# A four-layer transformer kernel: transposes a step behind their normalisation, the residual later, and the gated FFN's statistics and pieces placed elsewhere

## The chip, the cores and the metric

The kernel runs on one core of a Trainium2 chip. The metric is the device time of one execution in microseconds (us). The core has five engines that matter here: TensorE (PE, with its weight loads PEld), VectorE (DVE), ScalarE (ACT), GpSimd (POOL), and SyncE (SP), whose queue issues the DMA transfers. Each engine runs its own instructions in its program's order and waits on semaphores for the others.

## The reference

The input x has 2 sequences of 2048 rows of 256 floats (4096 rows). Four residual layers follow each other, each on a layer norm of the rows:

```python
x = x + A(layernorm(x))   # pre-norm attention, 16 heads of 16 over 4 key heads, causal window 64, rope; then FFN 256-1024-256 with gelu
x = x + B(layernorm(x))   # two layers of local attention and gated FFN
x = x + C(layernorm(x))   # gated attention unit: silu(uv), relu(q k + bias)**2, linear
x = x + D(layernorm(x))   # linear with a weight quantised to -1, 0, 1

# A(x): h = ln(x) * g1 + b1; x = x + attention(h) @ Wo + bo
#       x = x + gelu((ln(x) * g2 + b2) @ Wf1 + bf1) @ Wf2 + bf2
# a layer of B, twice:
h = shift_token(x)                   # second half of the columns from the row before
q, k, v = split(h @ wqkv, 3)         # 8 heads of 64
q, k = rotary_xpos(l2norm(q) * qs, l2norm(k) * ks)
x = x + local_attention(q, k, v) @ wo            # window 128, looks one window back
h = layernorm(shift_token(x)) * lg + lb
a, g = split(h @ w1 + b1, 2)         # 682 each
x = x + (a * gelu(g)) @ w2 + b2
```

All of it is in 32-bit floats.

## The kernel before, in words

**Tiling.** The rows are 32 tiles of 128 (NT). Four tiles make a group (GT = 4, NG = 8); a whole group is loaded, normalised and put through an FFN together. The rows stay on the chip in R through stage B; weights are loaded stage by stage.

**Steps.** Stages A and B are each a software pipeline in steps, one tile a step. A table says what each step holds: at(step, what, ...) appends an entry, and step_a and step_b write out the instructions of one step from its entries. For tile t, the projection to q, k, v stands in step t, scores in t+1, softmax weights (A: attend) in t+2, output (B: values and output) in t+3. In A, group g is loaded in step 4g-5, its statistics (means_of, L145 and L146) stand in 4g-3, and its normalisation in 4g-2. A's first layer norm is taken twice, the outer of the residual layer and the inner of the attention block: statistics_twice computes both scales in one POOL power (L161); normalised_twice makes h on DVE (L170); normalised_once makes y, the outer norm, which is the row sum that attention and FFN are added to, on DVE (L179) and ACT (L184); add_rows adds the bias bo to y on POOL (L207). to_features transposes h on PE (L215) and evicts it on ACT with gain and shift (L220); the projection (L380) reads that.

**FFN pieces.** When a group's attention is done, its FFN is prepared in step s = 4(g+1)+3: statistics, normalisation (A: L198), transposes. The products follow as pieces in later steps: in A eight hidden ones (L552) and four outputs (L563), in B six hidden (L1147, with the gate L1162 and L1163 on ACT and DVE) and four outputs (L1170, added by L1177). fill0, fill1 and fill2 are the places in a step where pieces stand. In A, finish closes a group five steps after s (the statistics and normalisation for B).

**Order.** The loop runs inside manual_schedule for PE, ACT, DVE and POOL: these four execute in the order in which step_a and step_b write their instructions. Only SP's queue, which carries the loads, is ordered by the framework's planner; in the trace SP issues transfers out of the program's order. The loop step is s; B's step is s - JOINT with JOINT = 35, so that A's tail (the last group's FFN) runs beside B's first steps. That is the joint A to B. Layer 1 of B starts GAP steps after layer 0's last tile: the joint of the layers.

**A step of B,** in the order of the program: values and their eviction (L1046, L1058 on PE; L1068 ACT, L1069 DVE); scores (L968), maxima (L980, L987 on DVE); exponentials (L999, ACT); projection (L893, PE), its evictions (L905, L907, ACT); turn, the rotated halves' products (L914 and L917, POOL); rotate_mul (L937, DVE); norm: sum of squares (L929, DVE), maximum and power (L930 and L932, POOL); rotate_add (L940, DVE); fill0; scale_keys (L944, DVE); softmax division (L1007, L1010, DVE); output (L1075) and its add (L1080); transposes of the softmax weights (L1018, L1023) with their evictions (L1030, L1032); to_features of q and k (L949, PE), the second half of which reads what L944 wrote; fill1 and fill2. In a prepare step the Ffn's parts are added: shifted (four DMA transfers of the rows' second halves, one row on, and in layer 1 a load xr of the residual), statistics (L1113 to L1115 on DVE, then rstd_of: L135 and L137 on POOL), normalise (eight of L1123 on DVE), residual (L1131 on POOL, four adds, eight in layer 1) and to_features (L215).

The lines around which the prepare step turns:

```python
if "prepare" in todo:
    l, g = todo["prepare"][0]
    f = ffns[l, g] = Ffn(l, g, wts[l])
    sh = f.shifted(sh)
    f.statistics()
...
if f:
    f.normalise()
if p:
    p.rotate_mul(0)
```

Scratch memory is divided into regions by address (W_B, LOW, HIGH, W_A); tags that are given to the region low share it between stages.

Of the kernel before, what the change touches and what calls it, by code (L numbers as in the profile page):

```python
# [12 lines left out]
ALU = mybir.AluOpType  # L13
# [4 lines left out]
P = 128  # L18
# [3 lines left out]
GT = 4  # L22
# [23 lines left out]
def kernel(ctx: ExitStack, tc: tile.TileContext, I: dict, out: bass.AP):  # L46
# [102 lines left out]
    def statistics_twice(src):  # L149

        mv = means_of(src)
        ve = T(small, [P, 2, GT], "ve2")
        nc.vector.tensor_scalar_add(ve[:, 0, :], mv[:, :, 1], EPS)
        nc.vector.tensor_scalar(ve[:, 1, :], mv[:, :, 1], 1.0 + EPS, EPS * EPS, ALU.mult, ALU.add)
        rs = T(small, [P, 2, GT], "rs2")  # L160
        nc.gpsimd.tensor_tensor(  # L161
            rs, ve, mhalf[:, 0 : 2 * GT].rearrange("p (a b) -> p a b", a=2), ALU.pow
        )
        return mv, rs

    def normalised_twice(src, stats, dst):
# [38 lines left out]
    def add_rows(dst, rows):  # L205
        for t in range(GT):
            nc.gpsimd.tensor_add(dst[:, t, :], dst[:, t, :], rows(t))  # L207
# [61 lines left out]


    low = Region(LOW, HIGH)
    low_tags = {tag: low for tag in ("y1", "xr1", "h", "hT2", "G")}
    wa = Region(HIGH + 5184, W_A, 2, low_tags)
    ca = wa
# [4 lines left out]
    class GroupA:  # L279
# [10 lines left out]
        def normalise(self):  # L290
            self.h = T(wa, [P, GT, D], "h", 1)
            normalised_twice(self.xg, self.stats, self.h)
            self.y = T(wa, [P, GT, D], f"y{self.g % 3}", 1)
            normalised_once(self.xg, self.stats, self.y, residual=False)
            add_rows(self.y, lambda t: boA)

        def to_features(self):
# [293 lines left out]
        at(t + 2, "attend", t)  # L591
        at(t + 3, "output", t)
    for g in range(NG):
        at(GT * g - 5, "load", g)
        at(GT * g - 3, "statistics", g)
        at(GT * g - 2, "normalise", g)
        s = GT * (g + 1) + 3
        at(s - 1, "residual", g)
        at(s, "prepare", g)

        if g < NG - 1:
            for c in range(ADFF // P):
                at(s + 1 + c // 4, f"fill{c // 2 % 2}", g, "hidden", c)
            for tt in range(GT):
                at(s + 3 + tt // 2, f"fill{tt % 2}", g, "output", tt)
        at(s + 5, "finish", g)

    groups_a, tiles_a, ffns_a = {0: first_group}, {}, {}
    steps_a = steps
# [1 line left out]
    def step_a(todo):  # L611
# [37 lines left out]
        if q:  # L649
            q.scores()  # L650
            q.mask(0)
            q.mask(1)
        if p:
            p.project()
            p.take()
# [39 lines left out]
            o.add_output()  # L695
        if q:
            q.exponents()
        if m:
            m.to_features()
        if f:  # L700
            f.to_features()


    wC = Region(W_A, END)
# [78 lines left out]


    low = Region(LOW, HIGH)
    wb = Region(HIGH + 5120, W_A, 2, {tag: low for tag in ("sh", "xr", "h", "hT", "gl", "hh")})
    cb = kept
    wb.reserve("tab", [P, 4, GT, BHD])
# [391 lines left out]

    GAP = 2
    steps = {}

    def at(step, what, *args):
# [6 lines left out]
    for l in range(BL):  # L1193
        s0 = l * (NT + GAP)
        for t in range(NT):
            at(s0 + t, "project", l, t)
            at(s0 + t + 1, "scores", l, t)
            at(s0 + t + 2, "weights", l, t)
            at(s0 + t + 3, "values", l, t)
            if t % GT == 0:  # L1200
                at(s0 + t - 4, "tables", l, t // GT)
                at(s0 + t - 3, "begin", l, t // GT)
        for g in range(NG):
            s = s0 + GT * (g + 1) + 3
            at(s, "prepare", l, g)

            for step, place, what, i in (
                (1, 0, "hidden", 0), (1, 1, "hidden", 1), (2, 0, "hidden", 2), (2, 1, "hidden", 3),
                (3, 0, "hidden", 4), (3, 0, "hidden", 5), (3, 1, "output", 0),
                (4, 0, "output", 1), (4, 1, "output", 2), (4, 2, "output", 3),  # L1210
            ):
                at(s + step, f"fill{place}", l, g, what, i)
        at(s0 + NT - 1, "free_qkv", l)
        at(s0 + NT + 2, "free_wo", l)
        at(s0 + NT + 7, "free_ffn", l)
# [1 line left out]
        at((BL - 1) * (NT + GAP) + NT + 3 + i, "next_stage")  # L1217


    for c in range(ADFF // P):  # L1220
        at(s_a + 1 + c // 4, f"fill{c // 2 % 2}", None, NG - 1, "hidden", c)
    for tt in range(GT):
        at(s_a + 3 + tt // 2, f"fill{tt % 2}", None, NG - 1, "output", tt)

    weights = {}
    wts = {0: weights}
# [5 lines left out]
    def step_b(todo):  # L1232
# [16 lines left out]
            tabs[l, g] = load_tab(g, scales[l])  # L1249
        if "prepare" in todo:  # L1250
            l, g = todo["prepare"][0]
            f = ffns[l, g] = Ffn(l, g, wts[l])
            sh = f.shifted(sh)
            f.statistics()

        def fill(place):

# [22 lines left out]
        if q:  # L1280
            q.scores(0)
            q.scores(1)
            q.maxima(0)
            q.maxima(1)
            q.exponents(0, (0,))
        if p:
            p.project(0)
# [2 lines left out]
            p.turn(0)  # L1290
        if q:
            q.exponents(0, (1,))
        if f:
            f.normalise()
        if p:
            p.rotate_mul(0)
            p.take(1)
# [14 lines left out]
        if p:  # L1312
            p.scale_keys()
        if f:
            f.residual()
        for l, g in todo.get("tables", ()):
            scale_tab(tabs[l, g], scales[l])
# [28 lines left out]
            groups[l, g] = begin_b(g, groups[l, g - 1][1] if g else None)  # L1346
        for r in rest:
            r()
        for (l,) in todo.get("free_qkv", ()):
            if l + 1 < BL:  # L1350
                wts[l + 1] = load_qkv(l + 1)
# [12 lines left out]
    with tc.manual_schedule(engines=ENGINES):  # L1364
        for s in range(min(steps_a), JOINT + max(steps) + 1):
            if s in steps_a:
                step_a(steps_a[s])
            if GT < s < JOINT - 4:
                next(masks, None)
            if s == JOINT + s_a + 6:  # L1370
                nc.gpsimd.memset(hh[:, 5, :], 0.0)
            step_b(steps.get(s - JOINT, {}))

# [340 lines left out]
```

## Time and profile before

| | us |
|---|---|
| median of 3 runs (lowest, highest) | 2650.28 (2650.09, 2653.59) |
| the profiled execution | 2653.07 |
| its span | 2651.3 |
| busy in the span: PE | 2578.8 |
| DVE | 1617.3 |
| ACT | 1197.5 |
| POOL | 985.8 |

The mean granted TensorE clock is 0.99. Stage A fills the first 510 us, B's projection starts at 513.28, B's last add (L1177) is at 1865.7, and C with D follow to the end. In the profile's rows a line number is that of the kernel before; "out<-in" are the program's names; a bracket holds the idle time of the engine just ahead of the instruction and what ended it. A line of the waits names the engine, the waiting instruction's output and line, what it waited for, and then the total in us, the number of times and the longest. A window's row has its bounds, its length, the busy time of PE, PEld, DVE, ACT and POOL with instruction counts, the granted clock, the DMA engines' busy share and GB/s. A helper's line (L135, L145, L215, L220) can serve several callers.

### The profile page before, as it was taken

The page shows a single profiled execution, that of the slowest core. Times are in us where ns is not written, and L with a number is a line of the kernel's source. Part 1 is how long each engine was busy: PE and PEld are TensorE (multiplying, and loading weights), DVE is VectorE, ACT ScalarE, POOL GpSimd, SP SyncE. Part 2 cuts the span into 40 slices and gives each one's busy share as a digit, 9 for nine tenths or more (in the row PEclk, how much of TensorE's full clock was granted, in tenths as well). Part 3 has the DMA queues.
Part 4 walks back from the last instruction along what each step waited for, and adds up shares of the span by engine and source line. Part 5 has one row for each costly group of instructions (what it writes and reads, how often), then busy time and mean ns, then how long its engine had stood idle before and what let it go on. Part 6 is the DMA issues. An engine that isn't in the chain of part 4 may idle for free.

```text
span 2651.3 us, 51289 instructions
## 1 busy us (share of the span) xinstructions
PE 2578.8 (97%) x20130; PEld 1647.1 (62%) x20130; DVE 1617.3 (61%) x4357; ACT 1197.5 (45%) x2505; POOL 985.8 (37%) x1221
## 2 busy tenths in 40 slices
PE   6899999998999999999999999999999999999998
PEld 4577777666666666666666676666545445445567
DVE  6778777567766767756766677774433435434344
ACT  3555555375666666646666666663510001500000
POOL 5555555544434444434544545542200002300011
PEclk9999999998999999999999999999999999999999
DMA  5001111111000001111210111001100000100000
GB/s 170 17 31 32 32 39 32 47 33 51 25 19 23 25 25 29 41 35 41 77 32 23 29 33 37 25 17 58 40 8 4 6 7 12 44 0 6 5 10 13
DMA packets 73168, 82.02 MB, mean 31 GB/s; under 512 B 18829, under 2 KB 57056, under 8 KB 72672
## 3 DMA queue, kind: packets, MB, share of 16 engines
q1 hardware_dynamic: 72928, 78.75, 10.4%
q8 instruction: 160, 2.62, 0.4%
q14 instruction: 80, 0.66, 0.1%
HBM read 44.20 MB, written 10.50 MB: 21 GB/s over the span
## 4 chain that ended last, share of the span: by engine, by line
PE 87%; DVE 5%; POOL 4%; issue 3%; DMA 1%; ACT 0%; SPq 0%; POOLq 0%; DVEq 0%; ACTq 0%
PE ps L1567 16%; PE ps L893 10%; PE ps L1147 10%; PE ps L1170 5%; PE ps L1491 4%; PE ps L563 4%; PE ps L552 4%; PE ps L1075 4%; PE ps L968 3%; PE ps L1046 2%; PE ps L1510 2%; PE ps L1479 2%; PE ps L1469 2%; PE ps L949 2%; PE ps L476 2%
## 5 line engine op out<-in xcount | busy, mean ns | idle before, releaser
L1567 PE MATMUL ps<-room 128*128 128x512 f32 (+1 forms) x1152 | 463.2, 544 | 0.0
L1567 PEld LDWEIGHTS ps<-room 128*128 128x128 f32 x1152 | 217.8, 189 | 221.9 <-issue 214.7
L893 PE MATMUL ps<-room 128*128 128x512 f32 x768 | 346.8, 601 | 0.0
L999 ACT ACTIVATE room<-room,shift,rn 128x192 f32<-128x192 f32 x512 | 276.4, 548 | 78.8 <-DVE shift L987 78.8
L914 POOL TENSOR_TENSOR room<-room 128x256 f32<-128x256 f32 x128 | 107.8, 842 | 493.1 <-ACT room L905 493.1
L1147 PE MATMUL ps<-room 128*128 128x512 f32 x640 | 287.7, 593 | 0.4 <-ACT room L220 0.4
L1535 ACT COPY room<-ps 128x256 f32<-128x256 f32 x32 | 11.9, 370 | 587.9 <-PE ps L1533 587.9
L932 POOL TENSOR_TENSOR rn<-ss,mhalf 128x8 f32<-128x8 f32 x128 | 243.0, 1898 | 10.7
L893 PEld LDWEIGHTS ps<-room 128*128 128x128 f32 x768 | 140.8, 190 | 157.4 <-issue 149.2
L1497 DVE SCALAR_TENSOR_TENSOR room<-ps,room 128x512 f32<-128x512 f32 (+1 forms) x144 | 90.2, 627 | 206.4 <-PE ps L1491 206.4
L1147 PEld LDWEIGHTS ps<-room 128*128 128x128 f32 x640 | 118.8, 190 | 136.8 <-issue 132.0
L1520 POOL TENSOR_SCALAR veC<-mvC 128x1 f32<-128x1 f32 x32 | 7.2, 226 | 453.5 <-DVE mvC L1518 453.5
L1170 PE MATMUL ps<-room 128*128 128x256 f32 x768 | 173.6, 380 | 0.0
L980 DVE CUSTOM_DVE_ANT_0 room<-ps,room 128x192 f32<-128x192 f32 x512 | 152.2, 354 | 15.7 <-PE ps L968 15.4
L1170 PEld LDWEIGHTS ps<-room 128*128 128x128 f32 x768 | 144.3, 191 | 24.9 <-issue 6.9
L1010 DVE TENSOR_SCALAR room<-room,rdB 128x192 f32<-128x192 f32 x512 | 156.1, 369 | 4.5
L1163 DVE SCALAR_TENSOR_TENSOR room<-ps,room 128x512 f32<-128x512 f32 x96 | 72.1, 751 | 127.1 <-PE ps L1147 88.7
L466 POOL TENSOR_TENSOR room<-room,mxA 128x1024 f32<-128x1024 f32 x64 | 120.2, 1900 | 58.4 <-PE ps L428 45.4
L1491 PE MATMUL ps<-room 128*128 128x512 f32 (+1 forms) x288 | 133.4, 545 | 0.0
L929 DVE TENSOR_REDUCE ss<-room 128x8 f32<-128x512 f32 x128 | 81.7, 680 | 73.9 <-ACT room L907 73.9
L1075 PE MATMUL ps<-room 128*128 128x256 f32 x512 | 121.0, 379 | 0.0
L1075 PEld LDWEIGHTS ps<-room 128*128 128x128 f32 x512 | 97.3, 190 | 34.1 <-issue 22.7
(182 smaller groups left out, 5019.9 us busy)
## 6 DMA issues: line engine op xcount, KB each, us to landing
room<-room SPq DMA_DIRECT2D x144, 128.0 KB
room<-in_L_attn_x_dram SPq DMA_DIRECT2D x16, 512.0 KB
room<-in_rope_b_dram SPq DMA_DIRECT2D x16, 512.0 KB
xs<-room SPq DMA_DIRECT2D x8, 512.0 KB
room<-xs SPq DMA_DIRECT2D x8, 512.0 KB
room<-in_rope_c_dram SPq DMA_DIRECT2D x8, 512.0 KB
out_dram<-R SPq DMA_DIRECT2D x32, 128.0 KB
room<-in_L_ffn_w_dram SPq DMA_DIRECT2D x6, 640.0 KB
```

The lines of the kernel that those rows point to most:

```text
L466: nc.gpsimd.tensor_sub(Sh, Sh, mc.unsqueeze(2).to_broadcast([P, 2 * AG, P]))
L893: nc.tensor.matmul(pm, src[:, cols], self.w["wqkv"][:, k, part * BIN : (part + 1) * BIN], start=k == 0, stop=k == 1,)
L914: nc.gpsimd.tensor_mul(u2[:, :, 0:hd2], x[:, :, hd2:BHD], sin[:, :, 0:hd2].to_broadcast([P, BH, hd2]))
L932: nc.gpsimd.tensor_tensor(self.rn[part], ss, mhalf[:, 0:BH], ALU.pow)
L980: nc.vector.tensor_tensor_reduce(S[:, e, jj, :], sc[e][:, jj * KW : (jj + 1) * KW], self.mask[:, jj, :], 1.0, -3.0e38, ALU.add, ALU.max, t ...
L999: nc.scalar.activation(S[:, e, jj, :], S[:, e, jj, :], AF.Exp, bias=self.shift[half][:, a : a + 1], scale=self.rn[0][:, head : head + 1], ...
L1010: nc.vector.tensor_scalar_mul(S[:, e, jj, :], S[:, e, jj, :], rd[:, a : a + 1])
L1075: nc.tensor.matmul(pm[:, 0:D], self.oT[:, k, :], wo[:, k, :], start=k == 0, stop=k == BIN // P - 1)
L1147: nc.tensor.matmul(pm, w["w1"][:, k, half, c * P : (c + 1) * P], hT[:, k, :], start=k == 0, stop=k == KC - 1,)
L1170: nc.tensor.matmul(pm[:, 0:D], hh[:, c, tt * P : (tt + 1) * P], self.w["w2"][:, c, :], start=c == 0, stop=c == BNC - 1,)
L1491: nc.tensor.matmul(pm[:, 0:n], self.KT[:, J * P : (J + 1) * P], self.QT[:, q0 : q0 + n], start=True, stop=True,)
L1567: nc.tensor.matmul(acc[e][:, 0:n], self.V[:, J, e * P : (e + 1) * P], s2, start=J == 0, stop=J == TPS - 1,)
```

## The change

Stage A: both scales of the double norm are computed by two POOL powers, the inner one (for h) first. A group is loaded one step later. Its h is transposed in step 4g-1, after the scores and the first two masks and ahead of the projection, where it was at the end of step 4g-2; y is computed at the end of step 4g-1 and gets its bias at the end of 4g+1. The FFN's transposes stand in step s+1, where they were at the end of s. The last group's pieces, which run beside B's first steps, are spread over six steps instead of four, and its finish stands at s+8.

Stage B: GAP is 1. The shift transfers (and xr) are issued at the end of the step before the prepare step. In the prepare step the statistics stand behind the maxima, where they stood at its start, and normalise behind scale_keys, where it stood ahead of rotate_mul. One memset is a step later. Memory regions are reserved by tag accordingly.

```diff
@@ -158,9 +158,8 @@
         nc.vector.tensor_scalar_add(ve[:, 0, :], mv[:, :, 1], EPS)
         nc.vector.tensor_scalar(ve[:, 1, :], mv[:, :, 1], 1.0 + EPS, EPS * EPS, ALU.mult, ALU.add)
         rs = T(small, [P, 2, GT], "rs2")
-        nc.gpsimd.tensor_tensor(
-            rs, ve, mhalf[:, 0 : 2 * GT].rearrange("p (a b) -> p a b", a=2), ALU.pow
-        )
+        for a in (1, 0):
+            nc.gpsimd.tensor_tensor(rs[:, a, :], ve[:, a, :], mhalf[:, 0:GT], ALU.pow)
         return mv, rs
 
     def normalised_twice(src, stats, dst):
@@ -269,6 +268,8 @@
 
 
     low = Region(LOW, HIGH)
+    for tag in ("h", "y1", "xr1"):
+        low.reserve(tag, [P, GT, D])
     low_tags = {tag: low for tag in ("y1", "xr1", "h", "hT2", "G")}
     wa = Region(HIGH + 5184, W_A, 2, low_tags)
     ca = wa
@@ -290,8 +291,12 @@
         def normalise(self):
             self.h = T(wa, [P, GT, D], "h", 1)
             normalised_twice(self.xg, self.stats, self.h)
+
+        def residual(self):
             self.y = T(wa, [P, GT, D], f"y{self.g % 3}", 1)
             normalised_once(self.xg, self.stats, self.y, residual=False)
+
+        def add_bias(self):
             add_rows(self.y, lambda t: boA)
 
         def to_features(self):
@@ -591,19 +596,22 @@
         at(t + 2, "attend", t)
         at(t + 3, "output", t)
     for g in range(NG):
-        at(GT * g - 5, "load", g)
+        at(GT * g - 4, "load", g)
         at(GT * g - 3, "statistics", g)
         at(GT * g - 2, "normalise", g)
+        at(GT * g - 1, "turn", g)
+        at(GT * g + 1, "bias", g)
         s = GT * (g + 1) + 3
         at(s - 1, "residual", g)
         at(s, "prepare", g)
+        at(s + 1, "turn_ffn", g)
 
         if g < NG - 1:
             for c in range(ADFF // P):
                 at(s + 1 + c // 4, f"fill{c // 2 % 2}", g, "hidden", c)
             for tt in range(GT):
                 at(s + 3 + tt // 2, f"fill{tt % 2}", g, "output", tt)
-        at(s + 5, "finish", g)
+        at(s + 5 if g < NG - 1 else s + 8, "finish", g)
 
     groups_a, tiles_a, ffns_a = {0: first_group}, {}, {}
     steps_a = steps
@@ -650,6 +658,10 @@
             q.scores()
             q.mask(0)
             q.mask(1)
+        for (g,) in todo.get("turn", ()):
+            groups_a[g].to_features()
+        for (g,) in todo.get("turn_ffn", ()):
+            ffns_a[g].to_features()
         if p:
             p.project()
             p.take()
@@ -695,10 +707,10 @@
             o.add_output()
         if q:
             q.exponents()
-        if m:
-            m.to_features()
-        if f:
-            f.to_features()
+        for (g,) in todo.get("turn", ()):
+            groups_a[g].residual()
+        for (g,) in todo.get("bias", ()):
+            groups_a[g].add_bias()
 
 
     wC = Region(W_A, END)
@@ -783,6 +795,11 @@
 
 
     low = Region(LOW, HIGH)
+    low.reserve("sh", [P, GT, P], 2)
+    low.reserve("xr", [P, GT, D])
+    low.reserve("gl", [P, GN], 2)
+    low.reserve("h", [P, GT, D])
+    low.reserve("hT", [P, KC, GN])
     wb = Region(HIGH + 5120, W_A, 2, {tag: low for tag in ("sh", "xr", "h", "hT", "gl", "hh")})
     cb = kept
     wb.reserve("tab", [P, 4, GT, BHD])
@@ -1180,7 +1197,7 @@
 
 
 
-    GAP = 2
+    GAP = 1
     steps = {}
 
     def at(step, what, *args):
@@ -1202,6 +1219,7 @@
                 at(s0 + t - 3, "begin", l, t // GT)
         for g in range(NG):
             s = s0 + GT * (g + 1) + 3
+            at(s - 1, "shift", l, g)
             at(s, "prepare", l, g)
 
             for step, place, what, i in (
@@ -1217,10 +1235,12 @@
         at((BL - 1) * (NT + GAP) + NT + 3 + i, "next_stage")
 
 
-    for c in range(ADFF // P):
-        at(s_a + 1 + c // 4, f"fill{c // 2 % 2}", None, NG - 1, "hidden", c)
-    for tt in range(GT):
-        at(s_a + 3 + tt // 2, f"fill{tt % 2}", None, NG - 1, "output", tt)
+    for step, place, what, i in (
+        (1, 0, "hidden", 0), (1, 0, "hidden", 1), (1, 1, "hidden", 2), (2, 0, "hidden", 3),
+        (2, 0, "hidden", 4), (2, 1, "hidden", 5), (3, 0, "hidden", 6), (3, 0, "hidden", 7),
+        (3, 1, "output", 0), (4, 0, "output", 1), (5, 0, "output", 2), (6, 0, "output", 3),
+    ):
+        at(s_a + step, f"fill{place}", None, NG - 1, what, i)
 
     weights = {}
     wts = {0: weights}
@@ -1249,9 +1269,7 @@
             tabs[l, g] = load_tab(g, scales[l])
         if "prepare" in todo:
             l, g = todo["prepare"][0]
-            f = ffns[l, g] = Ffn(l, g, wts[l])
-            sh = f.shifted(sh)
-            f.statistics()
+            f = ffns[l, g]
 
         def fill(place):
 
@@ -1282,6 +1300,9 @@
             q.scores(1)
             q.maxima(0)
             q.maxima(1)
+        if f:
+            f.statistics()
+        if q:
             q.exponents(0, (0,))
         if p:
             p.project(0)
@@ -1290,8 +1311,6 @@
             p.turn(0)
         if q:
             q.exponents(0, (1,))
-        if f:
-            f.normalise()
         if p:
             p.rotate_mul(0)
             p.take(1)
@@ -1312,6 +1331,7 @@
         if p:
             p.scale_keys()
         if f:
+            f.normalise()
             f.residual()
         for l, g in todo.get("tables", ()):
             scale_tab(tabs[l, g], scales[l])
@@ -1346,6 +1366,9 @@
             groups[l, g] = begin_b(g, groups[l, g - 1][1] if g else None)
         for r in rest:
             r()
+        for l, g in todo.get("shift", ()):
+            f = ffns[l, g] = Ffn(l, g, wts[l])
+            sh = f.shifted(sh)
         for (l,) in todo.get("free_qkv", ()):
             if l + 1 < BL:
                 wts[l + 1] = load_qkv(l + 1)
@@ -1367,7 +1390,7 @@
                 step_a(steps_a[s])
             if GT < s < JOINT - 4:
                 next(masks, None)
-            if s == JOINT + s_a + 6:
+            if s == JOINT + s_a + 7:
                 nc.gpsimd.memset(hh[:, 5, :], 0.0)
             step_b(steps.get(s - JOINT, {}))
```

## The prediction

> **What bounds the kernel now.** I read three views in this order: the page's busy shares and chain (who carries the time), the windows by stretch (where that engine is idle), and the waits of PE (what ends the idle time). All durations below are of the profiled execution: span 2651.3 us, 2653.07 us with what lies around it, 2.8 us above the median of the three runs. I work out differences on that trace and set them on the median.
>
> ```profile
> PE 2578.8 (97%) x20130; PEld 1647.1 (62%) x20130; DVE 1617.3 (61%) x4357; ACT 1197.5 (45%) x2505; POOL 985.8 (37%) x1221
> PE 87%; DVE 5%; POOL 4%; issue 3%; DMA 1%; ACT 0%; SPq 0%; POOLq 0%; DVEq 0%; ACTq 0%
> ```
>
> PE is idle for 2651.3 - 2578.8 = 72.5 us; no edit touches a matmul's size, so that is all there is to win. The windows (length, then busy PE, PEld, DVE, ACT, POOL, granted clock, DMA share, GB/s) say where it lies:
>
> ```profile
> 0.00:35.00 35.00, 16.06 (x157) 9.90 (x158) 14.67 (x40) 7.07 (x14) 17.36 (x44) 0.92 0.62 187
> 35.00:70.00 35.00, 29.27 (x448) 20.08 (x447) 32.38 (x51) 20.69 (x35) 22.25 (x25) 0.98 0.47 137
> 525.00:660.00 135.00, 124.42 (x1275) 86.60 (x1272) 89.99 (x322) 82.05 (x206) 65.61 (x81) 0.94 0.16 41
> 660.00:1165.00 505.00, 504.45 (x4879) 340.74 (x4878) 342.37 (x1112) 323.00 (x743) 218.28 (x259) 1.00 0.10 27
> 1165.00:1310.00 145.00, 135.64 (x1252) 92.83 (x1252) 100.66 (x325) 86.06 (x206) 71.13 (x88) 0.98 0.20 58
> ```
>
> Inside layer 0 of B (660 to 1165) PE lacks 0.55 us of 505: it is full, and any wait that an edit puts there is paid whole. The idle time is at the start (18.9 + 5.7 us), at the joint A to B (10.6) and at the joint of B's layers (9.4), where the clock also falls. PE's waits at these places:
>
> ```profile
> PE ps L949 <- DVE room L940: 16.5, 6, 3.7
> PE ps L215 <- DVE room L170: 12.9, 4, 9.1
> PE ps L215 <- DVE room L198: 5.8, 6, 3.4
> ```
>
> So DVE is late for PE: transposes stand in PE's program right behind the normalisation that feeds them (L170, L198), and the to-features transposes of B (L949) wait for the rotation.
>
> **The change part by part, stage A.** Moving the h transposes from the end of step 4g-2 to step 4g-1, and the FFN's from s to s+1, takes out waits that show as PE idle. Nine us of the L170 row are the first L215 at 9.09, before which nothing can run. Step 7: PE stuck at L215 starves DVE for 0.65 + 0.49 us; 1.1 gained. Step 8: the L198 wait is 3.38 us at 102.00, but its hidden matmuls (L552, 108.91) come 7.4 us after the normalisation began, and DVE is the bound there (over 18.6 of each 20 us between 40 and 80); I take 2.2. Start: the pow (L161, 1.67 for 128x8) becomes two of 1.04 (L137), the first only 0.6 earlier, and the four ACT y instructions (2.07, at 11.44) leave the way of the eviction L220 (13.42) and of L380 (14.23); but step 1's load is issued at 24.67 and its statistics start at 32.26, so part of this runs into that load: 2.2, between 0 and 2.8. Sum 5.5. The POOL adds L207 (four of 0.7) go to step 4g+1; steady A is full (370.00 of 370), so they gain and cost nothing there as long as ACT's eviction keeps its slack of about 0.35. The x load moves a step later on SP's queue: it lands in 5 to 6 us, statistics follow a step (over 12 us) later; covered, at the price of DVE waiting if not.
>
> **Joint A to B.** Spreading the last FFN's pieces over six steps puts a matmul ahead of L949 in steps 5 and 6. Step 5 idles 1.53 + 1.02 and then runs 6.83 us at half clock; I count 2.5 + 0.9 there and 1.4 in step 6 (less half clock). Step 0 gains nothing: POOL's eight L207 (6.2 us) end at 517.1 and its turn (L914) starts then; the L215 in front of L893 was cover, not cause. Step 7 (first gated FFN): DVE waits 1.37 for the shift's DMA (below); with statistics later that wait goes, but the transposes of its FFN end as late as before: 0. Sum 4.8.
>
> ```profile
> 634.80 0.29 DVE L1114 BATCH_NORM_STATS2 st<-room 128x6 f32<-128x128 f32 x1 [1.37 <-DMA room<-R]
> ```
>
> **Joint of the layers.** With GAP 1, step 35 keeps a projection under it and one step's tail is filled: 1.4 to 2.4. Against it the first prepare step without pieces loses 0.7 to 1.7 as below. I take +0.7. Layer 1's wqkv is issued at 1121 and landed by 1137; with GAP 1 it is needed at 1149 instead of 1161: covered by 12 us. The shift DMAs move a step earlier in the program only: SP already issues them when the last add of the rows is done. The memset moves by a step: one POOL instruction, nothing.
>
> **The steady prepare steps of B.** This is where I see a loss. Six groups in each layer (g 1 to 6) are prepared under a full PE: 12 steps. POOL and DVE rows of one such step (1033.25 on) and of the next, undisturbed one:
>
> ```profile
> 1036.29 0.23 POOL L135 TENSOR_SCALAR ve<-mv 128x4 f32<-128x4 f32 x1 [9.72 <-DVE mv L1115]
> 1036.61 1.04 POOL L137 TENSOR_TENSOR rs<-ve,mhalf 128x4 f32<-128x4 f32 x1
> 1039.09 0.64 POOL L914 TENSOR_TENSOR room<-room 128x256 f32<-128x256 f32 x1 [1.45 <-ACT room L905]
> 1044.24 1.67 POOL L932 TENSOR_TENSOR rn<-ss,mhalf 128x8 f32<-128x8 f32 x1
> 1046.32 0.69 DVE L944 TENSOR_TENSOR room<-room,rn 128x512 f32<-128x512 f32 x1
> ...
> 1059.95 0.69 DVE L937 TENSOR_TENSOR room<-room 128x512 f32<-128x512 f32 x1 [0.47 <-ACT room L905]
> 1059.99 1.15 POOL L914 TENSOR_TENSOR room<-room 128x256 f32<-128x256 f32 x1 [8.66 <-ACT room L905]
> ```
>
> Before, statistics use DVE's idle time ahead of L1069, and POOL has done L135 and L137 1.45 us before the turn may start. After, they follow the maxima. Count from x, the start of L1069. In the undisturbed step (x = 1056.08) the maxima end at x+3.4 and L914 starts at x+3.9. In the changed step the statistics take 2.4 (to x+5.8), and POOL, in program order, holds the turn behind L135 and L137 (0.23 + 1.04, to x+7.3). Then come four turns (2.55, to x+9.8), L930 (0.25) and L932 (1.67, to x+11.8), then L944 (0.69): x+12.5. PE reaches the half of L949 that reads L944 at x+12.5 (1047.7 less 1035.15, the x which PE sets when the statistics are away). Uncontended, the stall is 0.05.
>
> But they meet. The rows show 1.15 for an L914 started 0.04 us after an L937, and 0.64 without one. L135 would now start beside L937, a turn beside the second L937 and another beside L940: two or three hits of 0.5 us, so L944 ends between x+13.5 and x+13.9 and the stall is 0.95 to 1.35. [...] I take 1.2. Behind L944 on DVE, L1123 (eight, 2.6 us alone) now holds up L1010, L1177, L1080 and the eviction L1030, for which the next step's values wait; beside L1131 on POOL I get L1030's end at about 22.3 us into the step against a PE that, 1.2 late, wants it at 22.2: no second stall, but no slack. 12 x 1.2 = 14.4; bounds 0.6 and 12 x 1.7 = 20.
>
> **The clock.** A short idle can cost more. At the joint, a window with 1.53 us idle was followed by half clock:
>
> ```profile
> 609.85:613.26 3.41, 1.60 (x13) 1.15 (x11) 3.06 (x6) 3.41 (x14) 3.24 (x5) 1.00 0.00 0
> 613.26:620.09 6.83, 6.09 (x91) 5.67 (x94) 3.95 (x14) 3.52 (x8) 2.63 (x4) 0.50 0.01 3
> ```
>
> [...] By this row (1.60 busy of 3.41) a stall not much longer than 1.2 can trip it, at 1.7 us each (half of 3.41). The stretch 534.75 to 538.17 had 1.79 busy and stayed at full clock, so 1.2 us alone is mostly below the edge: I take 3 us in all, 0 to 20.
>
> **Sum.** Gains 5.5 + 4.8 + 0.7 = 11.0; losses 14.4 + 3 = 17.4; net 6.4 slower: 2659.5 for the profiled execution, 2650.3 + 6.4 = 2656.7 on the median. About 0.2% (5.3 us) is what a measurement here can tell from no change.
>
> **Rivals.** [...] DVE and POOL interleave so that L944 is in time: 12 x 0.05 = 0.6 lost, and the joints gain more (about 6 each, 5.5 in A, 17 in all): 16 us faster, 2634. For it: the uncontended walk ends 0.05 us late only, and L932 was not slowed. Against: the row with 1.15. *The clock trips in most prepare steps:* 14.4 + 12 x 1.7 - 11 = 24 slower, 2674. It decides from a stall of about 1.5 us in one window; against it, the 1.79-busy stretch. *They cancel:* stalls of 0.9 us lose 11, the gains are 11: 2650. The gains may also be smaller than said (the start behind its load): then 2659 to 2661, inside my own range.
>
> **How the numbers follow.** The forecast 0.52 (own range 2651 to 2665, 0.06 of it within 0.2%), no contention 0.25, clock 0.09, cancelling 0.14 (0.10 within, 0.02 on each side). Faster 0.25 + 0.02 = 0.27; same 0.06 + 0.10 = 0.16; slower 0.46 + 0.09 + 0.02 = 0.57. From 2634 to 2673 leaves out half of the two outer cases, 0.17.
>
> **What would show it.** In the changed profile: a new row in PE's waits, L949 behind L944, some 12 times at about 1.2 us; L135 right behind L1115 with L914 after L137 instead of after L905; PE below 498 of 505 in layer 0 of B. Right on the gains: no L215 wait on L170 or L198 but the first, and joint A to B idle at 6 us instead of 10.6. I am wrong if PE is as full in layer 0 as now (then faster), or if PE's clock falls below 0.98 in steady B (then far slower).

## The result: 35 us slower, and the profile after

The changed kernel takes 2686.96 us (median of 4 runs, 2684.66 to 2687.36) against 2651.94 for the kernel before in the same comparison: ratio 1.013, 95% interval 1.0113 to 1.0148. The forecast was 6.4 us slower, with a range that ended at 2673. The sign held; the size is more than five times too small. The profiled execution has a span of 2685.6 us, 34.3 more than the profiled one before.

Lines that moved or shifted have new numbers after the change. In B: L914 and L917 (turn) are L931 and L934, L937 is L954, L940 L957, L944 L961, L949 L966, L893 L910, L932 L949, L1123 L1140. L1115 is L1132, L930 L947, L1046 L1063. In A: L220 is L219, L184 L183, L179 L178, L207 L206, L406 L411, L421 L426, L552 L557, L427 L432. The helper's L215 is L214; L135 and L137 stay.

The page's busy shares and the windows of the changed kernel:

```profile
PE 2582.3 (96%) x20130; PEld 1646.0 (61%) x20130; DVE 1618.6 (60%) x4357; ACT 1206.6 (45%) x2509; POOL 1007.6 (38%) x1237
...
125.00:495.00 370.00, 361.13 (x4019) 256.37 (x4007) 281.09 (x551) 198.79 (x301) 205.73 (x238) 1.00 0.10 32
525.00:660.00 135.00, 120.47 (x1178) 82.70 (x1178) 89.29 (x298) 86.86 (x208) 78.31 (x92) 0.95 0.19 54
660.00:1165.00 505.00, 493.56 (x4826) 335.01 (x4823) 344.59 (x1138) 320.13 (x739) 226.02 (x262) 0.99 0.11 27
1165.00:1310.00 145.00, 141.74 (x1271) 94.54 (x1272) 90.33 (x284) 85.90 (x193) 63.29 (x75) 0.99 0.18 49
```

PE's busy time is almost the same (2582.3 against 2578.8). The time is in its idle time: 103.3 us instead of 72.5. In the window 660 to 1165, most of layer 0 of B and full before, PE now lacks 11.4 us of 505; in steady stage A, full before, it lacks 8.9 of 370. Of PE's largest waits two are new, L966 on L961 and L557 on L219. That of L432 on L426 has grown, and that of L966 on L957 has shrunk (16.5 before, as L949 on L940). After the dots stand the rows of the kernel before for the first and the second line; L557 on L219, as L552 on L220, was 0.4 once:

```profile
PE ps L966 <- DVE room L961: 32.8, 16, 3.2
PE ps L432 <- DVE room L426: 11.7, 6, 5.2
PE ps L557 <- ACT room L219: 9.2, 7, 1.7
PE ps L966 <- DVE room L957: 8.1, 4, 5.0
...
PE ps L949 <- DVE room L944: 1.5, 1, 1.5
PE ps L427 <- DVE room L421: 4.9, 5, 2.5
```

To place them I compared the starts of the projections, tile by tile, in the two traces. How far the changed kernel is behind the kernel before (minus: ahead):

| up to | behind by, us | gained or lost in the stretch |
|---|---|---|
| A, step 2 | -3.3 | -3.3 |
| A, step 8 | 1.5 | +4.8 |
| A, step 31 | 13.4 | +11.9 (six groups) |
| B, tile 9 of layer 0 | 10.8 | -2.6 (joint A to B) |
| B, tile 30 of layer 0 | 19.6 | +8.8 (five prepare steps) |
| B, tile 8 of layer 1 | 23.6 | +4.0 (joint of the layers) |
| B, tile 31 of layer 1 | 32.9 | +9.3 (five prepare steps) |
| end | 34.3 | +1.4 |

Stage A's first steps differ from execution to execution: of the runs below, those with the changed kernel's stage A unaltered end it 11.2 to 14.2 us behind the kernel before. A difference of 1 or 2 us that arises there says little. In the steady steps of B, traces of equal steps agree to about 0.2 us.

**A steady prepare step of B**, in the timeline of the changed kernel (POOL, then DVE, then PE):

```profile
1058.70 0.56 POOL L135 TENSOR_SCALAR ve<-mv 128x4 f32<-128x4 f32 x1 [14.48 <-DVE mv L1132]
1059.34 1.04 POOL L137 TENSOR_TENSOR rs<-ve,mhalf 128x4 f32<-128x4 f32 x1
1060.35 1.10 POOL L931 TENSOR_TENSOR room<-room 128x256 f32<-128x256 f32 x1
...
1062.61 1.09 POOL L934 TENSOR_TENSOR room<-room 128x256 f32<-128x256 f32 x1
1063.78 0.75 POOL L947 TENSOR_SCALAR ss<-ss 128x8 f32<-128x8 f32 x1
1064.61 1.67 POOL L949 TENSOR_TENSOR rn<-ss,mhalf 128x8 f32<-128x8 f32 x1
...
1058.53 0.64 DVE L954 TENSOR_TENSOR room<-room 128x512 f32<-128x512 f32 x1
...
1060.27 0.68 DVE L954 TENSOR_TENSOR room<-room 128x512 f32<-128x512 f32 x1
1062.08 1.11 DVE L957 TENSOR_TENSOR room<-room 128x512 f32<-128x512 f32 x1 [1.13 <-POOL room L934]
1063.73 0.69 DVE L957 TENSOR_TENSOR room<-room 128x512 f32<-128x512 f32 x1 [0.53 <-POOL room L934]
1066.31 0.69 DVE L961 TENSOR_TENSOR room<-room,rn 128x512 f32<-128x512 f32 x1 [1.89 <-POOL rn L949]
...
1067.15 0.63 PE L966 MATMUL ps<-ident,room 128*128 128x128 f32 x4 [1.71 <-DVE room L961]
```

The first bracket shows the queue: L135 waits for the statistics (L1132), and L137 and the turn follow it without a gap, so nothing on POOL started before 1058.70. DVE then waits for POOL three times. Four POOL operations are longer than at other places of the same trace (in brackets): L135 0.56 (0.23), the first L931 1.10 (0.64), the last L934 1.09 (0.64), L947 0.75 (0.25). They are as long, within 0.01, in all fifteen prepare steps that have a projection. Each of them starts while a 128x512 TENSOR_TENSOR runs on DVE: the first two beside L954, the last two beside L957. That is 1.7 us together, as much as PE waits. The wait is 1.70 to 1.72 in each of the twelve steps that prepare groups 1 to 6 of a layer. Ten of these steps lie in the steady stretches of the table; by the tile starts such a step costs 1.9 to 2.0 in eight of them and 1.2 to 1.3 in two, where the kernel before lost 0.55 itself, at its own L949. In the three prepare steps at the joints (655.9, 1221.2 and 1325.1 us) the same wait is 3.2: PE has a group of matmuls less ahead of L966 there (no L1187 in two, no L1092 in one) and comes to it earlier.

**A step of A in which an FFN's pieces begin** (ACT, then PE):

```profile
234.90 2.08 ACT L183 ACTIVATE room<-room,sh,rs 128x256 f32<-128x256 f32 x4 [4.82 <-DVE sh L178]
236.88 1.43 ACT L219 ACTIVATE room<-ps,room 128x512 f32<-128x512 f32 x2
...
237.69 3.70 PE L557 MATMUL ps<-room 128*128 128x512 f32 x8 [1.69 <-ACT room L219]
```

y of the next group, put at the end of step 4g-1, is the last thing on ACT ahead of the FFN transposes' eviction, and it waits for a DVE operation (L178) that stands behind that step's other work. PE waits 1.7 us in five such steps (175 to 426 us), and each step costs 1.9 to 2.0; in the first, at 111.7, the wait is 0.3.

### The profile page after: what moved, and what is told of

The parts are those of the page before. It is cut to its first block, busy times and chain, and to the rows that moved or that the text cites. A ratio compares the mean times of both kernels' runs of the same rounds, so it can differ in the third digit from the quotient of the medians.

```text
span 2685.6 us, 51308 instructions
## 1 busy us (share of the span) xinstructions
PE 2582.3 (96%) x20130; PEld 1646.0 (61%) x20130; DVE 1618.6 (60%) x4357; ACT 1206.6 (45%) x2509; POOL 1007.6 (38%) x1237
## 4 chain that ended last, share of the span: by engine, by line
PE 84%; DVE 7%; POOL 6%; issue 1%; ACT 1%; DMA 0%; SPq 0%; DVEq 0%; POOLq 0%; ACTq 0%
PE ps L1590 16%; PE ps L1164 10%; PE ps L910 9%; PE ps L1187 5%; PE ps L1514 4%; PE ps L557 4%; PE ps L568 3%; PE ps L1092 3%; PE ps L985 3%; PE ps L1063 3%; PE ps L1533 2%; PE ps L1502 2%; PE ps L966 2%; PE ps L1492 2%; PE ps L1035 2%; PE ps L481 2%
## 5 line engine op out<-in xcount | busy, mean ns | idle before, releaser
L1590 PEld LDWEIGHTS ps<-room 128*128 128x128 f32 x1152 | 217.8, 189 | 221.9 <-issue 214.7
L910 PE MATMUL ps<-room 128*128 128x512 f32 x768 | 346.6, 601 | 0.0
L1164 PE MATMUL ps<-room 128*128 128x512 f32 x640 | 287.6, 593 | 0.4 <-ACT room L219 0.4
L931 POOL TENSOR_TENSOR room<-room 128x256 f32<-128x256 f32 x128 | 112.9, 882 | 450.6 <-ACT room L922 450.6
L1558 ACT COPY room<-ps 128x256 f32<-128x256 f32 x32 | 11.8, 370 | 587.7 <-PE ps L1556 587.7
L949 POOL TENSOR_TENSOR rn<-ss,mhalf 128x8 f32<-128x8 f32 x128 | 241.6, 1888 | 10.7
L910 PEld LDWEIGHTS ps<-room 128*128 128x128 f32 x768 | 140.7, 190 | 157.4 <-issue 152.4
L1164 PEld LDWEIGHTS ps<-room 128*128 128x128 f32 x640 | 118.8, 190 | 137.3 <-issue 131.8
L1187 PE MATMUL ps<-room 128*128 128x256 f32 x768 | 174.7, 382 | 0.0
L1187 PEld LDWEIGHTS ps<-room 128*128 128x128 f32 x768 | 144.9, 192 | 25.3 <-issue 4.1
L557 PE MATMUL ps<-room 128*128 128x512 f32 x256 | 116.6, 598 | 9.2 <-ACT room L219 9.2
L1092 PE MATMUL ps<-room 128*128 128x256 f32 x512 | 121.0, 379 | 0.0
```

Source lines behind the costliest of these rows:

```text
L557: nc.tensor.matmul(pm, wf1[:, k, c * P : (c + 1) * P], self.hT[:, k, :], start=k == 0, stop=k == KC - 1)
L910: nc.tensor.matmul(pm, src[:, cols], self.w["wqkv"][:, k, part * BIN : (part + 1) * BIN], start=k == 0, stop=k == 1,)
L949: nc.gpsimd.tensor_tensor(self.rn[part], ss, mhalf[:, 0:BH], ALU.pow)
L1092: nc.tensor.matmul(pm[:, 0:D], self.oT[:, k, :], wo[:, k, :], start=k == 0, stop=k == BIN // P - 1)
L1164: nc.tensor.matmul(pm, w["w1"][:, k, half, c * P : (c + 1) * P], hT[:, k, :], start=k == 0, stop=k == KC - 1,)
L1187: nc.tensor.matmul(pm[:, 0:D], hh[:, c, tt * P : (tt + 1) * P], self.w["w2"][:, c, :], start=c == 0, stop=c == BNC - 1,)
```

## Experiments

Each experiment changes the kernel after the change unless its heading says otherwise. Times are medians, with the median of the kernel before in the same comparison (2651.6 to 2652.6).

**B's order undone, all else kept.**

```diff
-            f.statistics()      # behind the maxima
-            f.normalise()       # behind scale_keys
+            f.statistics()      # at the step's start
+            f.normalise()       # ahead of rotate_mul
```

> The changed kernel with B's statistics back at the start of the prepare step and its normalisation back in front of rotate_mul; all else as changed (shift a step earlier, GAP 1, pieces, stage A). If the order within the prepare step is the whole of B's loss (9.7 us in layer 0 and 9.3 in layer 1 by the step starts), 18 to 24 us faster than the changed kernel: 2663 to 2669, PE full in layer 0. If GAP or the earlier shift transfers carry part of it, less than 14 us (over 2673).

Measured: 2652.14 (ratio to before 0.9998, 0.9989 to 1.0007): 34.8 us come back, more than either theory gave. Layer 0 and layer 1 show no steady loss any more, and of the waits of L966 on L961 one is left, which is no prepare step's:

```profile
PE ps L966 <- DVE room L961: 2.7, 1, 2.7
```

By tile starts the order cost 18 us in the ten steady steps, 4 at the joint A to B, 10 at the joint of the layers and 2 at the end; the last steady step of each layer falls into the last two. The joints' own edits were gaining there all the time: with the order undone, 6.5 us at the joint A to B and 6.0 at the layers'. They had been hidden by the loss in the prepare steps of the joints, where L966 waits 3.2 us.

**B's order alone, on the kernel before.**

> The kernel before with only B's order changed: statistics behind the maxima, normalisation behind scale_keys (shift transfers, GAP, pieces and stage A as before). If the order is the loss by itself: 12 x 1.9 = 19 to 23 us slower than before, 2670 to 2675. If it only costs with the other edits: under 8 us slower.

Measured: 2684.49 (ratio 1.0122, 1.0107 to 1.0137), 32 slower. The order loses without the other edits, more than I expected. By tile starts the ten steady steps hold 18 of the 32; the two joints and the tail hold 13. PE's wait, in the lines of the kernel before, is that of the changed kernel:

```profile
PE ps L949 <- DVE room L944: 31.9, 16, 3.2
```

**rstd last on POOL.**

```diff
-            self.rs = rstd_of(mv)        # in statistics()
...
             p.norm(1)
             p.norm(0)
+        if f:
+            f.scale()                    # self.rs = rstd_of(self.mv)
```

> The changed kernel with one thing moved: in a prepare step of B the two POOL operations that make rstd (L135, L137) are issued behind turn and norm instead of in front of them; the DVE statistics stay behind the maxima. Theory (POOL's order): the turn starts at x+3.9 again, L961 is in time, and the 1.9 us that each of 10 to 12 prepare steps loses goes; 15 to 20 us faster than the changed kernel (about 2668), no wait of L966 on L961 in steady steps. Rival (DVE's own work): the 2.4 us of statistics between the maxima and the rotation make L961 late whatever POOL does; then under 5 us come back (over 2682). A second rival, that normalisation now late for want of rstd makes the next step's values wait, gives between 2670 and 2680 with a new wait on L1047.

Measured: 2672.67, 14.3 faster than the change. The POOL theory holds for layer 0, where a step now loses 0.3 us instead of 1.9; in layer 1 it still loses 1.7. The waits of PE say what took over there:

```profile
PE ps L214 <- DVE R L1196: 8.9, 6, 1.6
...
PE ps L214 <- DVE room L1142: 8.1, 8, 2.7
```

The FFN's transposes (L214) wait for the normalisation (L1142 in this kernel) at the first prepare step of each layer, and in layer 1's other steps for an add behind it on DVE (L1196): the normalisation now waits for its rstd behind both norms. The second rival had the right size (2670 to 2680) and the right cause, a normalisation that comes late; but PE waits at other lines than it named.

**rstd between the two norms.**

```diff
             p.norm(1)
+        if f:
+            f.scale()
             p.norm(0)
```

> The changed kernel with rstd's two POOL operations between the norm of k and the norm of q (behind turn, two operations earlier than in the run that put them last). If layer 1's remaining loss of 1.7 us a step in that run is the late normalisation (L214 waits for L1142 and for the FFN's last add, L1196, behind it on DVE), it goes down by about 1.9 us on POOL: 5 to 9 us faster than that run, 2664 to 2668. If the loss is DVE's own work, no change: 2672.

Measured: 2652.01 (ratio 1.000, 0.9992 to 1.0009): 20.7 us faster than with rstd last, and all 35 us of the change's loss are gone, with the statistics still behind the maxima on DVE. The rival that DVE's own work is the loss falls. I had expected 5 to 9; both waits of the run above went, the joints' included. POOL and DVE in a prepare step of this kernel:

```profile
1043.85 0.64 POOL L931 TENSOR_TENSOR room<-room 128x256 f32<-128x256 f32 x1 [12.47 <-ACT room L922]
...
1047.77 1.67 POOL L949 TENSOR_TENSOR rn<-ss,mhalf 128x8 f32<-128x8 f32 x1
1049.52 0.33 POOL L135 TENSOR_SCALAR ve<-mv 128x4 f32<-128x4 f32 x1
1049.93 1.51 POOL L137 TENSOR_TENSOR rs<-ve,mhalf 128x4 f32<-128x4 f32 x1
...
1047.87 0.68 DVE L954 TENSOR_TENSOR room<-room 128x512 f32<-128x512 f32 x1
1048.47 1.28 DVE L957 TENSOR_TENSOR room<-room 128x512 f32<-128x512 f32 x2
1049.86 0.69 DVE L961 TENSOR_TENSOR room<-room,rn 128x512 f32<-128x512 f32 x1
1051.48 0.35 DVE L1142 TENSOR_SCALAR room<-R,mv,rs 128x128 f32<-128x128 f32 x1 [0.93 <-POOL rs L137]
```

The turn starts at its own data (ACT's L922) again, beside the statistics on DVE, and its first operation is undisturbed (0.64). L961 waits for nobody and ends at 1050.6, and PE's L966 comes at 1051.99 with no wait. L1142 waits 0.93 for rstd without a wait of PE behind it. POOL and DVE still meet (L137 takes 1.51 instead of 1.04), but PE no longer waits for it.

**No L954 in prepare steps.**

```diff
-                p.rotate_mul(0)
+                p.rotate_mul(0, f)       # with f: u1 = raw, no product
```

(and the same for part 1)

> The changed kernel without L954 in B's prepare steps (the rotation's product with the cosine is left out in one tile of four; the sum takes the raw values). DVE already waits for POOL behind it (1.13 us at L957, 1.89 at L961), so its own time is not what this removes. Contention theory: L135 (0.56) and the first L931 (1.10) run at their undisturbed 0.23 and 0.64, the chain on POOL gets 0.8 us shorter, and the stall of 1.9 us at L966 falls to about 1.1: 8 us in the ten steady steps and 1 to 3 at the joints, 2675 to 2679. Rival, the queue's order alone with durations that nothing on DVE changes: 0 to 2 us, over 2684.

Measured: 2678.45, 8.5 faster than the change: the contention theory's number. The kernel leaves the product out and computes a different result. In its steady prepare steps L135 takes 0.23 and the first L931 0.64, and PE's wait is 0.91 to 0.93 in each of the twelve, 0.79 less, which is the 0.33 + 0.46 that the two operations got shorter. (In layer 1 another 0.3 appears at L214, so a step loses 1.1 in layer 0 and 1.6 in layer 1.) The other 0.9 of the stall stays, and so do the two long operations beside L957 (L960 in this kernel), which it keeps:

```profile
1056.47 1.09 POOL L934 TENSOR_TENSOR room<-room 128x256 f32<-128x256 f32 x1
1057.65 0.75 POOL L947 TENSOR_SCALAR ss<-ss 128x8 f32<-128x8 f32 x1
```

That these two are the other 0.9 (0.45 + 0.50) is worked out from their lengths; no run takes L957 away.

**A's y right behind the normalisation.**

```diff
         if m:
             m.normalise()
+            m.residual()
...
-        for (g,) in todo.get("turn", ()):
-            groups_a[g].residual()
```

> The changed kernel with stage A's y (L178 on DVE, four L183 on ACT) computed right after the normalisation in step 4g-2, not at the end of step 4g-1; its bias stays at the end of 4g+1. Theory: in step 4g the eviction L219 of the FFN's transposes is queued on ACT behind L183 (2.08 us) and L557 waits 1.7 us for it; this goes six times, 11 to 12 us faster (about 2675), no wait of L557 on L219. Rival: L557 waits because transposes and first product now stand in one step, whatever ACT does before; then under 3 us (over 2684).

Measured: 2678.08, 8.9 faster. A's tile starts stay at 1.5 to 1.6 us behind from step 9 to 31, and PE's wait is left once:

```profile
PE ps L557 <- ACT room L219: 0.4, 1, 0.4
```

The loss of 1.95 per group is gone, 9.9 us from step 9 to 31, so it was ACT's queue and not the distance of the transposes. At B's first projection the run is 11.8 us ahead of the change; 2 of that are given back at the joints and behind them, by the tile starts. I had expected 11 to 12 in the time.

**B's order and y undone, and the bias one step earlier.**

```diff
-        at(GT * g + 1, "bias", g)
+        at(GT * g, "bias", g)
```

> The changed kernel with B's order in the prepare step as before, stage A's y back in step 4g-2, and its bias (four L206 on POOL) at the end of step 4g, not of 4g+1. By the runs so far the first two add: 2652.1 - 8.9 = 2643. The bias is my theory for the loss of 4 us between A's steps 2 and 3: in the first group its 2.8 us on POOL stand between the power of group 1 and the rotation of step 2 (L408, L411), on which PE waits 5.2 us. If so, 2639 to 2641, and A's step 3 starts 3 us earlier than in the changed kernel. If that wait comes from group 1's load (2.2 us wait of DVE), the bias changes nothing: 2643.

Measured: 2642.23 (ratio 0.996, 0.9945 to 0.9975), 1 us less than the order and y give together (2643) and short of the 2 to 4 that I had expected of the bias; the time by itself doesn't tell the two theories apart. The tile starts do for the start: A's step 3 starts 3.0 us ahead of the kernel before, where the changed kernel is 0.6 behind and the run with B's order back 1.6. But from step 14 on each group loses 0.6 to 0.7 us, so that the gain is gone by step 31. The run above, with y at the same place and the bias at 4g+1, has no such loss from step 9 on, so in these groups the earlier bias costs it. In the changed kernel's start POOL shows why the bias matters:

```profile
36.05 2.77 POOL L206 TENSOR_TENSOR room<-room 128x256 f32<-128x256 f32 x4
...
39.44 0.51 POOL L411 TENSOR_TENSOR room<-room 128x160 f32<-128x160 f32 x1
...
39.98 0.42 DVE L421 TENSOR_TENSOR room<-room 128x256 f32<-128x256 f32 x1 [3.19 <-POOL room L411]
```

Before, these four adds stood ahead of the first rotation's POOL operations and waited 6.65 us for the bias's own load; now they stand ahead of the third's.

**The joints' edits alone, on the kernel before** (GAP 1, shift a step earlier, the pieces spread).

> The kernel before with the joints' edits alone: GAP 1, the shift transfers a step earlier, the last group's pieces of A spread over six steps; stage A and the order in B's prepare step as before. From the step starts of the run with B's order back, the joints gain 3 + 6.5 at A to B less what follows, and 6 to 7 at the layers': 2637 to 2641, 12 us faster than before. If the joints gain only because A's steps left room, 2645 to 2652.

Measured: 2636.96 (ratio 0.9943, 0.9926 to 0.9959): 14.7 us faster than before. 7.7 come from the joint A to B and 9.0 from the layers' (by tile starts of the profiled executions, whose spans differ by 16.7). GAP 1, the earlier shift and the spread pieces were not run apart from each other.

**The same, with the last eight adds of A later on POOL.**

> The joints-only kernel with one more move: the last group's eight bias and residual adds of stage A's FFN (L206 on POOL, 6.6 us, in front of B's first turn) are issued at the end of B's step 1, ahead of the first output piece. PE idles 7.7 us in B's step 0 behind POOL; if these adds are the cause, 4 to 7 us faster than the joints alone. If PE then waits for DVE or the DMA at the same place, under 1.5 us.

Measured: 2638.11, no gain. POOL is free, but its turn in B's step 0 now waits for ACT, which waits for PE, which has the FFN's transposes ahead of the projection:

```profile
516.81 1.15 POOL L934 TENSOR_TENSOR room<-room 128x256 f32<-128x256 f32 x1 [4.66 <-ACT room L925]
```

L934 is the turn in this kernel. Two waits end at nearly the same time there (in the run of the joints alone POOL comes free for the turn at 517.12; here the turn starts at 516.81); moving one alone gives nothing.

**The start's edits for the groups that need them.**

> The joints-only kernel plus the part of stage A's edits that pays at the start: h of every group transposed in step 4g-1, the two powers with h's first, group 0's y at the end of step -1, the bias of groups 0 to 2 at the end of step 4g; later groups' y and bias and all FFN transposes as before. By the step starts of the earlier runs A's step 9 then starts 3 us earlier and nothing is lost in the later steps: 2633 to 2635. If the turn in 4g-1 costs in the steady steps, 2637 to 2642.

Measured: 2650.11, 13 us slower than the joints alone. ACT shows it:

```profile
32.12 2.07 ACT L183 ACTIVATE room<-room,sh,rs 128x256 f32<-128x256 f32 x4 [20.38 <-DMA room<-in_L_attn_x_dram]
```

The load of group 1 stands in step -1, ahead of y of group 0, and both use one buffer: y waited for that load and took the wrong rows, so the time is that of a kernel with another result. That is what the load's later step is for in the change; my prediction had counted it as covered and no more.

**The same with the late transposes and adds at B's step 0.**

> The kernel of the run beside it, with the last group's FFN of stage A changed at B's step 0: its transposes stand behind B's first projection and its eight adds on POOL at the end of B's step 1. With the adds alone later nothing was gained, as the turn then waited for the projection behind the transposes; with both moved, 2 to 4 us less than the run beside it. If the next wait (step 1's L966 on L957) takes it over, under 1 us.

Measured: 2646.32, 3.8 faster than the run beside it, with the same wait at the start and the same wrong rows. Both causes moved together pay.

**The last with the loads in step 4g-4.**

> The joints-only kernel with the start's edits and the late transposes and adds at the joint A to B, and with A's loads in step 4g-4. In the two runs before, the load of group 1 (step -1) stood ahead of group 0's y and both use one buffer: y then waited 20.4 us for that load on ACT (and took the wrong rows), and everything behind started 13 us late. With the load behind it: start 3 us ahead of the joints alone, joint A to B 2 to 3.4 us better, 2629 to 2633, 20 us faster than before. If the load's own landing then holds group 1's statistics (2.2 us wait in the changed kernel), 2633 to 2637.

Measured: 2631.22 (ratio 0.9925, 0.9912 to 0.9939), 20 us faster than the kernel before and 56 faster than the change, with the right rows again. It keeps the change's edits at the start and at both joints, with the bias of the first three groups earlier and the last FFN's eight adds later than in the change. The order in B's prepare step, the FFN transposes of A's other groups, the y of groups 1 to 7 and the bias of groups 3 to 7 are as they were before. The gain over the joints alone is 5.7 us; by the tile starts 2.5 us are stage A's (executions with equal stages differ about as much there), 4.3 the joint A to B's and 1.5 the end's, and 2.9 are given back at the joint of the layers.

## Why the prediction was right and wrong

The trace's 34.3 us are 27.9 more than the forecast 6.4. By the tile starts and the run with B's order undone, stage A accounts for 18.9 of that (13.4 lost against 5.5 gained). The order in B's prepare step accounts for about 15 (34 against 14.4 + 3 + 1.2), and the joints' own edits take about 6 off (12.5 gained against 6.7). So two steps of the prediction failed: the gain of stage A, which put y's cost in ACT's queue at nothing, and the loss from B's order, sized too small in the steady steps and counted once at the joints.

- **Steady prepare steps (12 x 1.2 = 14.4 forecast, 12 x 1.71 = 20.5 of PE's waits measured).** The mechanism was right, by every sign that I had named: the wait of L966 on L961, L135 right behind the statistics, the turn behind L137. The number of steps was right too. The term of the sum that was off is the stall: 1.70 to 1.72 in every step, not 1.2. I took the middle of two or three hits of 0.5, and there are four (L947 beside L957 was not on my list). L949 kept 1.67, the time of L932 in the prediction's row at 1044.24.
- **The prepare steps at the joints (0.7 to 1.7 once forecast, 9.5 of waits at L966 measured).** "Against it the first prepare step without pieces loses 0.7 to 1.7" was applied once, to the joint of the layers, and the joint A to B was put at 0 for the same step. Three prepare steps lie there and wait, 3.2 us each at L966, because PE comes to it earlier than in a steady step; smaller waits follow at L214 and L1063. Undoing the order gave 4 us at the joint A to B, 10 at the layers' and 2 at the end, two steady steps included.
- **The joints' own edits (4.8 and 1.4 to 2.4 forecast, 14.7 measured alone).** The forecast was too small, above all at the joint of the layers, where the run of these edits alone shows 9.0 by tile starts.
- **Stage A (5.5 gained forecast, 13.4 lost).** This is the largest error. I costed y where it left (the start) and not where it arrived: in ACT's queue right ahead of L219, which costs 9.9 us in five groups, and the run with y earlier took that back. That "they gain and cost nothing there as long as ACT's eviction keeps its slack of about 0.35" was said of the bias alone, with a condition that I did not check against y. The bias itself was not costed on POOL at the start: its new place stands ahead of the third rotation and takes back the start's 3.3 us. The rest, about 3 us between A's steps 3 and 9, has no cause shown.
- **The clock (3 forecast, 0 measured in steady B).** Stalls of 1.7 us in full steps did not trip it: between the first prepare step of layer 0 and the joint of the layers the granted clock of the changed kernel is 1.00. Behind the 3.2 us waits of the first prepare step of each layer it is half for 10.24 us, where the prediction had put nothing:

```profile
655.69:665.93 10.24, 8.40 (x132) 7.34 (x136) 8.95 (x29) 2.51 (x4) 5.30 (x7) 0.50 0.11 25
666.00:1222.00 556.00, 542.47 (x5146) 364.27 (x5139) 373.75 (x1223) 352.62 (x809) 251.61 (x291) 1.00 0.10 27
1324.70:1334.94 10.24, 7.25 (x105) 6.19 (x108) 8.54 (x22) 2.52 (x4) 7.38 (x9) 0.50 0.19 57
```

The 3.41 us just ahead of the two rows of half clock hold 0.41 and 0.62 us of PE's work; a stall of 1.7 us leaves half of such a stretch busy. With the order undone (mean granted clock of the profiled execution 0.991, against 0.987) there is no half clock at the first of these places and 3.41 us at the second, and PE is busy for 6.5 us less with the same instructions (2575.8 against 2582.3). So part of the order's cost at the joints is probably the clock; how much, no run separates. For the steady steps the stretch that the prediction had set against its row (534.75 to 538.17, 1.79 us busy, full clock) was nearer than the row (1.60 busy of 3.41, then half clock).

- **The rivals.** No contention: ruled out, since without L954 the stall shrank by the two hits (0.33 + 0.46). The clock: ruled out for the steady steps by the middle row above; its 24 us were nearer to the time, for the wrong reason, which is luck. That all cancels: no, the order lost some 34 us and the joints gained 12.5.

## What to carry to other kernels

An operation that is moved costs where it arrives, on its own queue: list what stands behind it there, on every engine that it uses, and not only what it releases where it leaves. Two small operations on an in-order queue (1.3 us here) that wait for data can cost some 35 us when the operations behind them feed the bound engine, and placing them six instructions later on that queue took all of it back. Price a stall in every step that has it, the ones at the joints first: there the bound engine has less work ahead of the wait (3.2 us of stall against 1.7 here).

## What the hardware showed that I had not expected

Two very short POOL operations took two to three times as long when they started beside a running 128x512 TENSOR_TENSOR of DVE: L135 0.56 instead of 0.23 beside L954 (0.23 again in the run without L954), and L947 0.75 instead of 0.25 beside L957. A POOL power that was already running kept its 1.67, and the DVE operations that started beside it kept their usual time (in the run with rstd between the norms L949 at 1047.77, an L954 of 0.68 at 1047.87, two L957 in 1.28). A power that started 0.07 us behind L961 in the same step took 1.51 instead of 1.04. And PE waits of 1.7 us in steady B left the granted clock at 1.00, where waits of 3.2 us at the first prepare step of each layer had half clock for 10.24 us behind them.
